# Four convolution layers on one core: layer 2's 3x3 convolution takes both halves of a tile in one 128x128 band

## The chip, the cores and the metric

The kernel runs on one core of a Trainium2 chip. TensorE (PE) does matrix products, VectorE (DVE), ScalarE (ACT) and GpSimd (POOL) do elementwise work, and SyncE (SP), ACT and GpSimd issue transfers (DMA). The metric is the device time of the whole program in microseconds (us), as a median of several executions. Times in the profile are counted from the span's start.

## The reference

The input x has 4 time steps (T), 8 channels (B), and images of 512 x 512. Four residual layers follow each other, each `x = x + f(groupnorm(x))`. Layer 0 is a spiking attention block, layer 1 a 13x13 depthwise convolution. This case is about layers 2 and 3:

```python
    def _L2_conv_ref(x, weight, bias):
        ...
        sx = MAX_Q / jnp.max(jnp.abs(x))
        sw = MAX_Q / jnp.max(jnp.abs(weight))
        qx = _quantize(x, sx)
        qw = _quantize(weight, sw)
        out_i32 = lax.conv_general_dilated(qx, qw, ..., padding=[(1, 1), (1, 1)], ...)
        out = out_i32 / (sx * sw)
        return out + bias[None, :, None, None]
    ...
    x = x + _L2_conv_ref(_gn(x), L2_conv_weight, L2_conv_bias)
    x = x + _L3_conv_ref(_gn(x), L3_conv_weight, L3_conv_bias)
```

Both are 3x3 convolutions with 8 input and 8 output channels. Layer 2 works on integers up to 127, layer 3 in float32. Between the two stands a group norm, whose statistics need the whole of layer 2's result for one time step.

## The kernel before

Layers 0 and 1 leave their result in device memory, one array for each time step, with a row of the image and a channel as its rows (`x2d`). Layers 2 and 3 run together, in `layers23`.

**Windows and tiles.** An image's 512 rows are cut into 85 windows of 8 rows that start every 6 rows (`W_IN`, `W_STEP`, `W_ALL`), so that neighbours share two rows. A window has 8 rows x 8 channels = 64 partitions, and two windows stand above each other in a tile of 128 partitions: half a = 0 and half a = 1. Two tiles (j = 0 and 1) make a pair, with four windows; `place` says where each stands: windows 4p and 4p+1 are the halves of tile j = 0, windows 4p+2 and 4p+3 the halves of tile j = 1, the even one of the latter in half 1. There are 22 pairs for a time step, and 88 in all.

**Layer 2** (`layer2`, L1051) convolves along the rows by three products, one for each horizontal tap dx, that add up in PSUM. The vertical taps and the channels are in the weights: a band matrix `band2` of 64 x 64 for each half. So each half of a tile is a product of its own, from its 64 partitions to its 64 partitions of PSUM, and of a window's 8 rows only the inner 6 come out right, as the outer two lack a neighbour. L1058 (DVE) scales the result, adds the residual and writes it to `x3`, a ring of 26 pairs in SBUF. Sums and squares for the next norm are taken on DVE (L1058's accumulator, L1069) and ACT (L1064).

**Halos** (`halos`, L1207). Before layer 3 can convolve, each window's outer rows must be overwritten by the right ones, which the neighbouring window has. For every boundary of two windows a row of 8 channels is copied in each direction, from SBUF to SBUF, by transfers that GpSimd issues. For 11 pairs (`n_chunk`) at a time, the copies of all boundaries of one kind c (c = 0 to 3: the boundary ahead of window 4p + c) are one transfer in each direction, or two where the ring wraps. They are spread over the following iterations, one or two in each.

**Layer 3** (`layer3`, L1153) is again three taps times the halves of a tile, 64 x 64, in float32, of which TensorE makes two passes each. L1162 (ACT) adds the constant, and SyncE writes the tile out (L1169). Before the products, GpSimd sets the two columns at the image's edges (L1146).

**The loop.** One iteration n loads pair n + 5 (L1002, SyncE), brings pair n + 2 into order and scales it (`normalise`: L1016 on POOL, L1020 on ACT), rounds pair n + 1 to bf16 (`quantise`: L1031 on DVE), runs layer 2 of pair n, issues halos, and runs layer 3 of pair n - 25. After a time step's last pair, `norm3` (L1104 to L1135) makes the norm's constants and layer 3's weights from the statistics, a few steps in each iteration. Buffers: six for loads (`x`), four for `u`, two for `y`, ten for outputs (`o`). SyncE's queue holds loads and outputs in one order. The order on each engine is made by a scheduler from the program's order, with `tc.issue_after` to hold layer 2 behind the normalising of later pairs and layer 3 behind layer 2.

**Weights.** `weights23` builds the bands while layer 1 runs, with small products (L891) and copies (L896).

Of the kernel before, what the change touches and what calls it, by code (L numbers as in the profile page):

```python
# [33 lines left out]
F32 = mybir.dt.float32  # L34
BF16 = mybir.dt.bfloat16
# [7 lines left out]
P = 128  # L43
T, B, N, D, H = 4, 8, 512, 512, 8
# [20 lines left out]
W_IN, W_STEP, W_ALL = 8, 6, 85  # L65
N_PAIRS = (W_ALL + 3) // 4
W2_N = 2 * N_PAIRS - 1
HALF = P // 2
# [4 lines left out]
def place(q):  # L73

    p, c = divmod(q, 4)
    return p, c // 2, (c % 2) ^ (c // 2)


def windows(k):

    p, j = divmod(k, 2)
    every = [(a, 4 * p + 2 * j + (a ^ j)) for a in range(2)]
    return [(a, q) for a, q in every if q < W_ALL]
# [43 lines left out]
def network(ctx: ExitStack, tc: tile.TileContext, i: dict, out: bass.AP):  # L127
# [115 lines left out]
    with ExitStack() as s:  # L243
        ps_1 = s.enter_context(pool("ps_2", space=PSUM))
        layer1 = Layer1(
            s, tc, x1d, x2d, avg, group_stats, r1, mr1, st2, m2, r2, most, w_sum, head, ps_1, pool
        )
        layer1.group(0)
        for g in range(1, G):
            if g == 1:  # L250
                with ExitStack() as behind:
                    for op in layer1.started:
                        behind.enter_context(tc.issue_after(op))
                    norm1(G - 1, ps_1)
                    w23 = weights23(tc, i, late, early["y"], ps_1, ident)
            layer1.group(g)
        layer1.next_norm(G - 1)
# [603 lines left out]
def weights23(tc, i, pool, scratch, ps_1, ident):  # L861


    nc = tc.nc

    def col(name, n=1):
        return pool.tile([P, n], F32, name=name)

    n_taps = 3 * B
    w = {}  # L870
    c24 = pool.tile([n_taps, i["c24"].shape[1]], F32, name="c24")
    nc.scalar.dma_start(c24, i["c24"])
    w2 = pool.tile([n_taps, n_taps], F32, name="w2t")
    nc.scalar.dma_start(w2, i["w2"])
    w3 = pool.tile([n_taps, n_taps], F32, name="w3t")
    nc.scalar.dma_start(w3, i["w3"])
    w["b2"], b3 = col("b2"), col("b3")
    nc.scalar.dma_start(w["b2"], i["b2"])
    nc.scalar.dma_start(b3, i["b3"])
    w["b23"] = col("b23")  # L880
    nc.vector.tensor_add(w["b23"], w["b2"], b3)

    def banded(taps, dtype, name, firsts):

        band = pool.tile([P, len(firsts), 3, HALF], dtype, name=name)
        for b, first in enumerate(firsts):
            ps = ps_1.tile([P, W_IN, n_taps], F32, tag="misc", name=f"ps_{name}")
            for row in range(W_IN):
                at = (W_IN - first - row) * B
                for a in range(2):  # L890
                    nc.tensor.matmul(  # L891
                        ps[a * HALF : (a + 1) * HALF, row, :], lhsT=c24[:, at : at + HALF],
                        rhs=taps, start=True, stop=True,
                    )
            for dx in range(3):
                nc.vector.tensor_copy(  # L896
                    band[:, b, dx, :].rearrange("p (r c) -> p r c", c=B),
                    ps[:, :, dx * B : (dx + 1) * B],
                )
        return band  # L900

    w["band3"] = band3 = banded(w3, F32, "band3", (-1, 1))
    w["sum3"] = pool.tile([P, 2, HALF], F32, name="sum3")
    nc.vector.tensor_add(w["sum3"], band3[:, :, 0, :], band3[:, :, 1, :])
    nc.vector.tensor_add(w["sum3"], w["sum3"], band3[:, :, 2, :])
    w["eye3"] = pool.tile([P, 2, 3, HALF], F32, name="eye3")
    nc.vector.memset(w["eye3"], 0.0)
    nc.vector.tensor_add(  # L910
        w["eye3"][:, 0, 1, B:], ident[:, : HALF - B], ident[:, HALF : P - B]
    )
    nc.vector.tensor_add(
        w["eye3"][:, 1, 1, : HALF - B], ident[:, B:HALF], ident[:, HALF + B :]
    )

    wall = scratch.tile([P, 2, D], F32, tag="y", name="wall")
    wall = wall.rearrange("p n d -> p (n d)")[:, : n_taps * n_taps]
    nc.scalar.dma_start(wall, bass.AP(i["w2"].tensor, 0, [[0, P], [1, n_taps * n_taps]]))
    w["sw"] = sw = col("sw")  # L920
    nc.vector.tensor_reduce(sw, wall, AX.X, ALU.max, apply_absolute_value=True)
    nc.vector.reciprocal(sw, sw)
    nc.vector.tensor_scalar_mul(sw, sw, MAX_Q)
    nc.vector.tensor_scalar_mul(w2, w2, sw[:n_taps])
    nc.vector.tensor_scalar(w2, w2, MAX_Q, -MAX_Q, op0=ALU.min, op1=ALU.max)
    nc.vector.tensor_scalar(w2, w2, ROUND, ROUND, op0=ALU.add, op1=ALU.subtract)
    w["band2"] = banded(w2, BF16, "band2", (0,))


    w["xq"] = [pool.tile([P, 2, D + 4], BF16, name=f"xq_{j}") for j in range(3)]  # L930
    for xq in w["xq"]:
        nc.gpsimd.memset(xq, 0.0)
    w["st3"] = [pool.tile([P, W2_N, 6], F32, name=f"st3_{j}") for j in range(2)]
    for st3 in w["st3"]:
        nc.gpsimd.memset(st3, 0.0)

    w["sums"] = [pool.tile([P, 2, W2_N], F32, name=f"sums_{j}") for j in range(2)]
    w["inv"] = col("inv")  # L940
    w["m"], w["r"] = col("m_own", T), col("r_own", T)
    w["mr"] = col("mr_own", T)
    return w


def layers23(
    s, tc, x2d, out, ident, ind, mask2, avg_same, group_steps, m2, r2, most, w, early, pool
):
    nc = tc.nc
    ps_1 = s.enter_context(pool("ps_3", space=PSUM))  # L950
# [8 lines left out]
    ps = ps_1.tile([1, P], F32, tag="misc", name="ps_most")  # L959
# [7 lines left out]
    ps = ps_1.tile([P, 1], F32, tag="misc", name="ps_top")  # L967
# [18 lines left out]
    def tiles(p):  # L986
        return [k for k in (2 * p, 2 * p + 1) if k < W2_N]

    def slot(t, p):
        return 2 * ((t * N_PAIRS + p) % RING)  # L990
# [46 lines left out]
    def by_sums(t):  # L1037
        return range(0 if t == 0 else 1, W2_N - 1, 1 if t == 0 else 2)

    def layer2(t, p):  # L1040
        ks = tiles(p)
        n_p = HALF * len(windows(ks[-1]))
        u, xq = ready.pop((t, p))
        s0 = slot(t, p)
        st3 = w["st3"][t % 2]
        for j, k in enumerate(ks):
            ps = ps_2.tile([P, D], F32, tag="conv2", name="ps_conv2")
            for dx in range(3):
                for a, _ in windows(k):
                    half = slice(a * HALF, (a + 1) * HALF)  # L1050
                    mm = nc.tensor.matmul(  # L1051
                        ps[half, :], lhsT=w["band2"][half, 0, dx, :], rhs=xq[half, j, dx + 1 : dx + 1 + D],
                        start=dx == 0, stop=dx == 2,
                    )
            own = x3[:n_p, s0 + j, 1 : D + 1]
            sums = w["sums"][t % 2][:, :, k : k + 1]
            summed = k in by_sums(t)
            done["DVE"] = nc.vector.scalar_tensor_tensor(  # L1058
                own, ps[:n_p, :], w["inv"][:n_p], u[:n_p, j, :], op0=ALU.mult, op1=ALU.add,
                accum_out=sums[:, 0, :] if summed else None,  # L1060
            ).ins
            if summed:
                square = wpool.tile([P, D], BF16, tag="square", name="square")
                done["ACT"] = nc.scalar.activation(  # L1064
                    square, own, AF.Square, bias=w["m"][:, t : t + 1], scale=-1.0,
                    accum_out=sums[:, 1, :],
                ).ins
            else:
                done["DVE"] = nc.vector.bn_stats(st3[:n_p, k, :], own).ins  # L1069
        return mm.ins  # L1070
# [3 lines left out]
    def halos(t, p0, p1):  # L1074


        for c in range(4):
            first = max(p0, 1) if c == 0 else p0
            n = min(p1, (W_ALL - c + 3) // 4) - first
            _, j, a = place(c)  # L1080
            before, j_b, a_b = place(c + 3)
            for q0, q1, n_q in split(t, first, n, before - 1):
                here = pairs[a * HALF : (a + 1) * HALF, q0 : q0 + n_q, j, :]
                there = pairs[a_b * HALF : (a_b + 1) * HALF, q1 : q1 + n_q, j_b, :]
                end = (W_IN - 1) * B
                yield here[:B], there[W_STEP * B : (W_STEP + 1) * B]
                yield there[end : end + B], here[B : 2 * B]

    def split(t, p, n, back):

        while n > 0:
            q0, q1 = slot(t, p) // 2, slot(t, p + back) // 2
            now = min(n, RING - q0, RING - q1)
            yield q0, q1, now
            n, p = n - now, p + now
# [85 lines left out]
    for n in range(n_all + N_PAIRS + LAG):  # L1181
# [20 lines left out]
        if n_chunk < n <= n_all + 3 and n % n_chunk == 3:  # L1202
            t, p = divmod(n - 3 - n_chunk, N_PAIRS)
# [4 lines left out]
        if n >= N_PAIRS + LAG:  # L1208
            t, p = divmod(n - N_PAIRS - LAG, N_PAIRS)
# [41 lines left out]
```

## Time and profile before

The median is 3003.39 us (3001.87 to 3005.93, three runs); the profiled execution spans 3002.9 us.

| what | before |
|---|---|
| PE busy, of the whole span | 2889.0 us (96%) |
| layers 2 and 3 | from about 2563 us to the end |
| layer 2's products (L1051), 64x64 bf16 | 1020, 399 ns each |
| layer 3's products (L1153), 64x64 float32 | 2040, 612 ns each |
| halo issues (L1207) on POOL | 94, 57.8 us busy |
| `u` copies (L1016), 128x512, on POOL | 168, 1187 ns each |
| quantise (L1031), 128x1024, on DVE | 84, 1131 ns each |
| packets on GpSimd's queue (q0) | 23776, 62.35 MB |

How to read it: a product's duration is its whole way through the array, so products that follow each other or stand side by side overlap, and the distance of their starts tells what they cost. A group's line gives its count, its busy time, the mean of one and the idle time ahead of it, with what ended that. The chain of waits follows the work that ended last back to its start: only what stands on it sets the time. The DMA share is the mean busy share of the core's 16 DMA engines; packets that overlap can take it above 1.

### The profile page before, as it was taken

The page shows a single profiled execution, that of the slowest core. Times are in us where ns is not written, and L with a number is a line of the kernel's source. Part 1 is how long each engine was busy: PE and PEld are TensorE (multiplying, and loading weights), DVE is VectorE, ACT ScalarE, POOL GpSimd, SP SyncE. Part 2 cuts the span into 40 slices and gives each one's busy share as a digit, 9 for nine tenths or more (in the row PEclk, how much of TensorE's full clock was granted, in tenths as well). Part 3 has the DMA queues.
Part 4 walks back from the last instruction along what each step waited for, and adds up shares of the span by engine and source line. Part 5 has one row for each costly group of instructions (what it writes and reads, how often), then busy time and mean ns, then how long its engine had stood idle before and what let it go on. Part 6 is the DMA issues. An engine that isn't in the chain of part 4 may idle for free. (4 is left out here: it accounts for less than half of the span.)

```text
span 3002.9 us, 38667 instructions
## 1 busy us (share of the span) xinstructions
PE 2889.0 (96%) x13873; PEld 1426.6 (48%) x13873; DVE 2225.3 (74%) x3875; ACT 551.0 (18%) x859; POOL 1054.3 (35%) x1971
## 2 busy tenths in 40 slices
PE   7999999999999999999999999999999999588889
PEld 3545555555555555555555555555333333244334
DVE  7887788688779868867976886786656556896660
ACT  2200000011010001001000000110112112766664
POOL 3342233233234323323422333332211112776651
PEclk9999999999999999999999999999999999889999
DMA  5311212112222222211121111112878779698886
GB/s 193 107 61 60 82 57 70 65 64 71 71 64 64 65 64 73 70 65 64 64 65 57 43 51 57 50 49 65 215 196 220 211 199 251 134 201 210 223 199 174
DMA packets 278240, 327.75 MB, mean 109 GB/s; under 512 B 23639, under 2 KB 173855, under 8 KB 277935
## 3 DMA queue, kind: packets, MB, share of 16 engines
q1 hardware_dynamic: 212304, 236.70, 28.7%
q0 software_dynamic: 23776, 62.35, 7.5%
q10 hardware_dynamic: 41967, 26.23, 3.0%
q8 instruction: 109, 1.79, 0.2%
q14 instruction: 84, 0.69, 0.1%
HBM read 210.57 MB, written 103.60 MB: 105 GB/s over the span
## 5 line engine op out<-in xcount | busy, mean ns | idle before, releaser
L485 PE MATMUL ps_in<-w_v,xn 128*128 128x512 f32 x1024 | 461.7, 600 | 2.6 <-DVE w_kq L344 2.6
L485 PE MATMUL ps_in<-xn,w_kq 128*128 128x512 f32 x1024 | 453.0, 595 | 4.8 <-DVE v_q L441 3.7
L485 PE MATMUL ps_in<-w_kq,xn 128*128 128x512 f32 x1024 | 450.1, 593 | 1.6 <-DVE v_k L450 1.6
L797 PE MATMUL ps_conv<-x,bt 112*64 112x512 f32 x2048 | 445.3, 592 | 0.8 <-ACT xo L804 0.6
L521 PE MATMUL ps_b<-toep,vtok 128*64 128x512 bf16 x3072 | 371.3, 381 | 0.0
L433 ACT ACTIVATE h_q<-v_q,c_half 128x512 f32<-128x512 f32 x96 | 69.3, 722 | 1550.4 <-DVE v_q L429 1205.7
L570 POOL COPY x1s<-x1s 128x2 f32<-128x2 f32 (+1 forms) x1024 | 227.3, 276 | 299.2 <-DVE x1s L559 299.2
L548 PE MATMUL ps_out<-wp,so 128*128 128x512 f32 x1024 | 308.4, 443 | 0.0
L458 POOL TENSOR_TENSOR h_v<-h_v,c_v 128x512 f32<-128x512 f32 x96 | 123.2, 1283 | 513.4 <-DVE h_v L457 504.4
L485 PEld LDWEIGHTS ps_in<-w_kq,xn 128*128 128x128 f32 x1024 | 194.3, 190 | 223.1 <-issue 205.3
L485 PEld LDWEIGHTS ps_in<-xn,w_kq 128*128 128x128 f32 x1024 | 192.1, 191 | 227.4 <-issue 211.8
L1153 PE MATMUL ps_conv<-x,band_t 64*64 64x512 f32 x2040 | 276.1, 612 | 24.4 <-ACT o L1162 13.8
L485 PEld LDWEIGHTS ps_in<-w_v,xn 128*128 128x128 f32 x1024 | 190.7, 191 | 215.9 <-issue 210.8
L797 PEld LDWEIGHTS ps_conv<-x,bt 112*64 112x64 f32 x2048 | 147.6, 135 | 288.6 <-issue 286.3
L521 PEld LDWEIGHTS <-vtok 128*64 128x64 bf16 x3072 | 207.7, 110 | 123.6 <-issue 2.1
L548 PEld LDWEIGHTS ps_out<-wp,so 128*128 128x128 f32 x1024 | 192.6, 188 | 94.4 <-issue 57.8
L1016 POOL COPY u<-x 128x512 f32<-128x512 f32 (+1 forms) x172 | 198.2, 1185 | 104.5 <-DMA x<-x 56.7
L559 DVE SCALAR_TENSOR_TENSOR x1s<-v_p,xr 128x256 f32<-128x256 f32 x256 | 187.1, 771 | 16.2 <-DMA x<-x1s 5.2
L195 POOL TENSOR_TENSOR grstd_x<-grstd_x,neg_half 128x1 f32<-128x1 f32 (+1 forms) x28 | 21.3, 762 | 473.5 <-DVE grstd_x L194 473.5
L815 POOL DMA_DIRECT2D x<-xo x128 | 71.4, 565 | 312.4 <-ACT xo L804 298.1
L1153 PEld LDWEIGHTS ps_conv<-x,band_t 64*64 64x64 f32 x2040 | 112.3, 136 | 135.9 <-issue 94.2
L1051 PE MATMUL ps_conv<-xq,band 64*64 64x512 bf16 x1020 | 138.8, 399 | 32.1 <-DVE xq L1031 32.0
(182 smaller groups left out, 3580.4 us busy)
## 6 DMA issues: line engine op xcount, KB each, us to landing
x<-x SPq DMA_DIRECT2D x64, 917.0 KB
x<-x SPq DMA_DIRECT2D x168, 256.0 KB
x<-x1s POOLq DMA_DIRECT2D x128, 262.0 KB, 2.5
x<-in_x SPq DMA_DIRECT2D x128, 256.0 KB
xr<-in_x SPq DMA_DIRECT2D x128, 256.0 KB
out<-o SPq DMA_DIRECT2D x164, 192.0 KB
xs<-in_x SPq DMA_DIRECT2D x112, 256.0 KB
x<-xo ACTq DMA_DIRECT2D x128, 128.0 KB
```

The lines of the kernel that those rows point to most:

```text
L433: nc.scalar.activation(h, v, AF.Identity, bias=c_col, scale=0.5)
L458: nc.gpsimd.tensor_add(h, h, c_twice[n])
L485: mm = nc.tensor.matmul(ps, lhsT=lhsT, rhs=rhs, start=k == 0, stop=k == NC - 1)
L521: nc.tensor.matmul(pb[two * DH : (two + 1) * DH, :], lhsT=v[:, c, h * DH : (h + 1) * DH], rhs=toep[z][:, h, u : u + N], start=c == 0 and z ...
L548: nc.tensor.matmul(ps, lhsT=so[:, k, c * P : (c + 1) * P], rhs=wpT[z][:, k, :], start=k == 0 and z == 0, stop=k == NC - 1 and z == 1,)
L559: nc.vector.scalar_tensor_tensor(own, v.rearrange("p (g v) -> p g v", g=PH)[:, two, :], 1.0, by_phase[:, two, :], op0=ALU.is_ge, op1=ALU.add,)
L570: nc.gpsimd.tensor_copy(x1[:, f, u : u + n], x1[:, fm, um - n + 1 : um + 1][:, ::-1])
L797: mm = nc.tensor.matmul(ps[q * M1 : (q + 1) * M1, :], lhsT=bt[:, z, :], rhs=xt[:, w0 : w0 + N_PS1, z : z + NV], start=z == 0, stop=z == SH ...
L815: engine.dma_start(bass.AP(dst.tensor, dst.offset + (q * n_half * W1_OUT * B + b) * D + f * NV, [[B * D, W1_OUT], [W1_OUT * B * D, n_half] ...
L1016: nc.gpsimd.tensor_copy(u[:n_p, j, :].rearrange("p (v g) -> p v g", g=PH), x[:, j, :].rearrange("p (g v) -> p v g", g=PH),)
L1051: mm = nc.tensor.matmul(ps[half, :], lhsT=w["band2"][half, 0, dx, :], rhs=xq[half, j, dx + 1 : dx + 1 + D], start=dx == 0, stop=dx == 2,)
L1153: mm = nc.tensor.matmul(ps[j][b * HALF : (b + 1) * HALF, :], lhsT=band[half, b, dx, :], rhs=x3[half, s0 + j, dx : dx + D], start=dx == 0, ...
```

## The change

The weights of layer 2 become one band of 128 x 128 for each kind of tile (j = 0 and 1). Its diagonal blocks are the old 64 x 64 band, and the blocks beside the diagonal hold the taps by which the rows at the boundary of a tile's two halves see each other. A tile then takes one product of 128 x 128 for each dx instead of two of 64 x 64, and the boundary inside a tile comes out right without a copy. Copies are left for c = 0 and c = 2 alone: the boundaries between tiles. To make room, the taps and the old band now stand in a scratch tile (`parts`), and the new band is put together by more copies and four small products.

```diff
-    def banded(taps, dtype, name, firsts):
-
-        band = pool.tile([P, len(firsts), 3, HALF], dtype, name=name)
+    def banded(taps, band, name, firsts):
...
-    w["band2"] = banded(w2, BF16, "band2", (0,))
+    w["band2"] = band2 = pool.tile([P, 2, 3, P], BF16, name="band2")
+    nc.gpsimd.memset(band2, 0.0)
+    inner = banded(w2, inner.rearrange("p (b x m) -> p b x m", b=1, x=3), "inner2", (0,))
+    nc.vector.tensor_copy(below, w2)
+    nc.vector.memset(below[: 2 * B, :], 0.0)
+    ps = ps_1.tile([P, 2, n_taps], F32, tag="misc", name="ps_outer2")
+    for a in range(2):
+        half = slice(a * HALF, (a + 1) * HALF)
+        at = (W_IN - W_STEP) * B
+        nc.tensor.matmul(
+            ps[half, 0, :], lhsT=c24[:B, at : at + HALF], rhs=w2[:B, :], start=True, stop=True
+        )
+        at = (W_STEP + 1) * B
+        nc.tensor.matmul(
+            ps[half, 1, :], lhsT=c24[:, at : at + HALF], rhs=below, start=True, stop=True
+        )
+    for a in range(2):
+        half = slice(a * HALF, (a + 1) * HALF)
+        nc.vector.tensor_copy(
+            band2[half, :, :, half],
+            inner[half, 0, :, :].unsqueeze(1).to_broadcast([HALF, 2, 3, HALF]),
+        )
+        for j in range(2):
+            at = (1 - a) * HALF + (0 if j == a else HALF - B)
+            nc.vector.tensor_copy(
+                band2[half, j, :, at : at + B],
+                ps[half, 0 if j == a else 1, :].rearrange("p (x c) -> p x c", c=B),
+            )
...
             for dx in range(3):
-                for a, _ in windows(k):
-                    half = slice(a * HALF, (a + 1) * HALF)
-                    mm = nc.tensor.matmul(
-                        ps[half, :], lhsT=w["band2"][half, 0, dx, :], rhs=xq[half, j, dx + 1 : dx + 1 + D],
-                        start=dx == 0, stop=dx == 2,
-                    )
+                mm = nc.tensor.matmul(
+                    ps[:n_p, :], lhsT=w["band2"][:n_p, j, dx, :n_p],
+                    rhs=xq[:n_p, j, dx + 1 : dx + 1 + D], start=dx == 0, stop=dx == 2,
+                )
...
     def halos(t, p0, p1):
...
-        for c in range(4):
+        for c in (0, 2):
```

More of the change, by code (lines that the diff above doesn't have):

```diff
@@ L870, in weights23 @@
     w = {}
-    c24 = pool.tile([n_taps, i["c24"].shape[1]], F32, name="c24")
+    parts = scratch.tile([P, 2, D], F32, tag="y", name="parts")
+    c24 = parts[:n_taps, 0, : i["c24"].shape[1]]
     nc.scalar.dma_start(c24, i["c24"])
-    w2 = pool.tile([n_taps, n_taps], F32, name="w2t")
+    w2, w3, below = (parts[:n_taps, 1, j * n_taps : (j + 1) * n_taps] for j in range(3))
     nc.scalar.dma_start(w2, i["w2"])
-    w3 = pool.tile([n_taps, n_taps], F32, name="w3t")
     nc.scalar.dma_start(w3, i["w3"])
+    inner = parts[:, 1, P : P + 3 * HALF // 2].bitcast(BF16)
     w["b2"], b3 = col("b2"), col("b3")
@@ L900, in banded @@
         return band
-    w["band3"] = band3 = banded(w3, F32, "band3", (-1, 1))
+    band3 = pool.tile([P, 2, 3, HALF], F32, name="band3")
+    w["band3"] = banded(w3, band3, "band3", (-1, 1))
     w["sum3"] = pool.tile([P, 2, HALF], F32, name="sum3")
```

## The prediction

> **What bounds the kernel now.** I read the page's forty slices first, then the chain of waits in order of time, the groups by shape, the waits and some windows of the last third; only layers 2 and 3 are touched, and they run from 2563 us to the end. The slices:
>
> ```profile
> PE   7999999999999999999999999999999999588889
> DMA  5311212112222222211121111112878779698886
> ```
>
> Up to slice 34 TensorE is full; after it, PE has gaps and the transfers are near full. The chain, in order of time:
>
> ```profile
> 2653.53 2.58 PE ps_conv L1153 x22
> 2656.10 1.08 PE ps_conv L1051 x10
> 2657.19 0.21 PE ps_conv L1153
> 2657.40 2.58 PE ps_conv L1153 x22
> ...
> 2692.56 22.85 DMA out<-o x3
> ```
>
> From 2650 to 2692 the chain is TensorE alone, one pair of tiles every 2657.40 - 2653.53 = 3.87 us. Then it jumps to output transfers. The columns below are us, busy PE, PEld, DVE, ACT and POOL with their counts, granted clock, DMA share, GB/s:
>
> ```profile
> 2570.00:2600.00 30.00, 19.84 (x152) 8.19 (x150) 27.89 (x59) 28.69 (x57) 26.59 (x22) 0.94 0.60 159
> 2600.00:2630.00 30.00, 16.52 (x107) 6.16 (x104) 29.00 (x48) 25.73 (x51) 25.32 (x27) 0.85 1.00 149
> 2647.00:2692.00 45.00, 44.77 (x418) 22.18 (x418) 43.06 (x64) 36.57 (x59) 39.84 (x53) 0.98 1.04 208
> 2715.00:2930.00 215.00, 185.91 (x1586) 88.98 (x1586) 142.41 (x272) 139.35 (x223) 134.84 (x183) 0.95 0.87 210
> ```
>
> So there are four stretches. A, to 2650: layer 2 alone, ACT and DVE full. B, 2650 to about 2715: PE full, while transfers already take a share of 1.04 and fall behind. C, 2715 to 2930: the timeline of L1058 shows pairs 43 to 87, so 215 / 45 = 4.78 us a pair against PE's 3.87, and PE is idle for 29 us. D, the last 73 us: layer 3 alone on PE. What ends the waits in C (the waits of 2700 to 2930: total, times, longest):
>
> ```profile
> ACT o L1162 <- DMA out<-o: 64.2, 37, 6.3
> POOL u L1016 <- DMA x<-x: 44.7, 21, 6.0
> ```
>
> ACT waits for an output buffer to be written out, POOL for an input to land: C is bound by transfers.
>
> **What the halo copies cost.** The packet records of C, by queue: 1344 packets of 4096 B on GpSimd's queue (the halos), 557 ns each; 18998 of 2048 B on SyncE's queue (loads, outputs), 111 ns each. 1344 x 557 ns = 749 us; 18998 x 111 ns = 2109 us; the whole is 0.87 x 16 x 215 = 2993 us. Halos are 13% of the bytes but 25% of the time. The 2048 B packets take 152 ns in 2647:2692, where the share is 1.04, and 104 ns after 2940, with few halos.
>
> **What the Trainium skill says.** "DMA: Bandwidth & Descriptors", section "Issuing engines are not separate DMA queues": transfers of all issuing engines share the same 16 engines and interleave. The slower 2048 B packets beside halos agree. "SBUF — State Buffer", section "Who interferes with whom": a DVE instruction in a two-port mode and a GpSimd instruction exclude each other. The trace agrees; quantise takes 0.68 us when POOL is idle, 1.06 us beside its copies, and more when a halo issue has put POOL behind:
>
> ```profile
> 2610.05 3.28 DVE L1031 TENSOR_SCALAR xq<-y 128x1024 bf16<-128x1024 f32 x1 [0.18 <-ACT y L1020]
> 2614.59 0.68 DVE L1031 TENSOR_SCALAR xq<-y 128x1024 bf16<-128x1024 f32 x1
> ```
>
> "TensorEngine Tiling (Array Packing)", section "Key Properties": changing the tiling mode drains TensorE. The trace shows this at a norm, where a 128x128 product stands between 64x64 ones:
>
> ```profile
> 2732.03 1.03 PE L1051 MATMUL ps_conv<-xq,band 64*64 64x512 bf16 x8
> 2732.99 0.38 PE L178 MATMUL gps_x<-gsum_x,avg_same 128*128 128x1 f32 x2
> 2733.30 0.66 PE L1153 MATMUL ps_conv<-x,band_t 64*64 64x512 f32 x4
> ```
>
> Two 64x64 products run side by side every 0.215 us, so the last two of the eight start at 2732.03 + 3 x 0.215 = 2732.68; L178 starts 0.31 later instead of 0.215: 0.09 us for the switch.
>
> **The change, part by part.**
>
> 1. Layer 2 on PE. Before: 12 products of 64x64 a pair, two side by side, 6 x 0.215 = 1.29 us (the chain's 1.08 + 0.21). After: 6 full products, 6 x 0.215 = 1.29 us. No full bf16 product over 512 columns is in the trace. The nearest, L501 (128x128 bf16 over 128 columns), starts every 0.054 us, so its weights hide; L548 (f32 weights) takes 1.86 / 8 = 0.2325 us. Bounds 0.215 and 0.2325; I take 0.215, as bf16 weights hide. Zero here.
>
> 2. Mode switches, added. The built order keeps layer 2's 6 products and layer 3's 12 in turns, so each pair switches from 64x64 to 128x128 and back: 2 x 0.09. After a switch the first weights are not hidden: L1153's first product takes 0.641 instead of 0.588 us after L178 (+0.05); I take 0.03 to 0.05 for bf16. Together 0.26 to 0.28; bounds 0.2 and 0.4. Layer 2's first pairs have no layer 3 between them. It concerns pairs 25 to 87, where PE's floor becomes 3.87 + 0.28 = 4.15 us. In B (17 pairs) nothing hides it: +5 us. In C it adds 45 x 0.28 = 12.6 us, where 29 us of idle can take it.
>
> 3. Halos. Of 94 copies (10752 KB: 84 boundaries, two directions, 16 KB each, four time steps) 50 remain (5376 KB). In C this takes 749 / 2 / 16 = 23 us off each DMA engine: 187 - 23 = 164 us busy for 45 pairs, 3.6 us a pair at a share of 1. At C's share of 0.87 that is 4.2 us, about PE's new floor. C's bounds: 45 x 4.15 = 187 us if nothing else waits, 215 if the waits have another cause. In C before, the excess over the larger floor (187 us of transfers) was 28 us; after, the larger floor is PE's 187 and transfers have 23 us to spare, so I take half of that excess, 13 us: 200 us, 15 less than 215.
>
> 4. A. In the first chunk 4 instead of 8 halos are issued. The pair's period there is 2.54 us without halos and 9.28 for three pairs with them, so 1.66 us lost three times; I count one fewer: 1.7. The first norm begins with L1104, which waits 3.6 us behind POOL's copies and a halo issue (its neighbours of the same shape take 0.25): 3.3 back. In the new order DVE interleaves the norm with pairs 22 and 23, but then waits on PE and POOL in a row: about -0.5. Sum 4.5, bounds 0 and 7.
>
> 5. POOL's order. Edges (L1146), one a pair before, now stand in batches of up to 18 ahead of copies, some behind a halo's landing (6.7 us by the page's issues). The same work, but three bursts of some 4 us and a wait of up to 4 us each. Behind them stand the u copies, then ACT's y, quantise, layer 2. POOL is 135 of 215 us busy and works two pairs ahead, so I charge 1 us each, 3 in all; bounds 0 and 12.
>
> 6. Set-up. Four small products, six copies, a memset and a copy of the taps, in layer 1. The products cost PE under 0.3 us; DVE has idle time there (about 30 busy of 50 us), and L759's last three bands come 13.9 us (one image of L797) before PE needs them. Zero.
>
> D is untouched. Sum: A -4.5, B +5, C -15, POOL +3: -11.5, so 2992.
>
> **The rivals.** (a) Transfers get out of the way wholly: C falls to 187 us, POOL costs nothing, A gives 4.5: 3003.4 - 28 + 5 - 4.5 = 2976. For it: B before ran at PE's floor despite a share of 1.04, and halos come in bursts that buffers can take up. Against: norms at pairs 43 and 65 stall DVE anyway, and PE's products run at half speed for some us after an idle time. (b) The gains cancel: C gains only 4, which pays for B less A, and POOL 3: 3003. For it: loads and outputs stay (0.62 of the share of 0.87). (c) Slower: SyncE issues loads and outputs in one order, each waiting for buffers, so C's waits may be a matter of that order; then C keeps its 215, B pays 5, POOL up to 10, A gives 4.5: 3003.4 + 5 + 10 - 4.5 = 3014; with a switch at 0.4 us somewhat more. For it: SyncE's own waits are for ACT and POOL, not for transfers. Against: the share above 1 and the 557 ns packets.
>
> **How the numbers follow.** The main case (2982 to 2997) has 0.47, (a) 0.18, (b) 0.2, (c) 0.15. Faster by 0.2% means below 2997.4: main and (a), 0.65. Same: 0.2. Slower: 0.15. The range reaches from just above (a)'s floor, 2977, into (c), 3009.
>
> **What would show it.** Right: layer 2 as some 504 products of 128*128 (the four time steps' last tiles stay half) with nearly the duration of before and PE's chain near 4.15 us a pair in B; 50 halo issues; share in C near 0.85; waits of L1162 for out clearly under 64 us; L1104 under 1 us. Wrong: a period near 3.9 in B (switches cheap: faster than forecast), or C still at 4.7 us a pair with half the halos (transfers were not it).

## The result, and the profile after

| kernel | median us | lowest to highest | ratio to before, 95% interval |
|---|---|---|---|
| before | 3004.66 (4 runs) | 3001.87 to 3011.84 | |
| after | 2992.15 (4 runs) | 2990.54 to 2996.51 | 0.9957 [0.9936, 0.9978] |

The changed kernel is faster by 0.43%; the profiled executions span 3002.9 and 2991.6 us. Lines have moved by 29 or 31: L1051 is now L1080 (layer 2's products), L1153 L1182 (layer 3's), L1016 L1047 (`u` copies), L1020 L1051 (ACT's scaling to `y`; the number that layer 2's products had before), L1031 L1062 (quantise), L1058 L1087 (residual), L1104 L1133 (the norm's first step), L1146 L1175 (edges), L1162 L1191 (output), L1207 L1236 (halo issues).

Where the difference lies is seen from the starts of each pair's first L1058 or L1087 in the timeline (us; in brackets us a pair):

| stretch | before | after | difference | forecast |
|---|---|---|---|---|
| to pair 0 | 2571.24 | 2574.66 | +3.4 | 0 |
| A: pairs 0 to 25, layer 2 alone | 79.58 | 77.70 | -1.9 | -4.5 |
| B: pairs 25 to 43, PE full | 71.65 | 74.39 | +2.7 | +5 |
| C: pairs 43 to 87 | 207.66 (4.72) | 192.05 (4.36) | -15.6 | -15, and +3 for POOL's order |
| D: from pair 87 on, layer 3 alone | 72.81 | 72.81 | 0 | 0 |

The 3.4 us ahead of pair 0 are there in full after layer 0's second image (289.08 against 292.53 us), where both kernels do the same work, and the seven other kernels below that build the new band reach pair 0 at 2570.64 to 2575.26. So it varies from run to run and is not put down to the change. In layers 2 and 3 alone the profiles differ by -1.9 + 2.7 - 15.6 = -14.8 us.

The page's slices, after:

```profile
PE   7999999999999999999999999999999999689999
DMA  5312222222222221212221111111877778698865
```

Of the four slices near the end that stood at 8 before, three are at 9 now: TensorE is full to the end but for the norms. The windows of A's end and of C (us, busy PE, PEld, DVE, ACT, POOL with their counts, granted clock, DMA share, GB/s):

```profile
2647.00:2692.00 45.00, 43.72 (x301) 14.26 (x308) 38.67 (x58) 32.52 (x53) 38.68 (x58) 0.95 0.97 211
2715.00:2930.00 215.00, 205.38 (x1446) 68.65 (x1465) 170.63 (x294) 144.07 (x233) 134.99 (x178) 0.99 0.79 198
```

In C, PE is idle for 215 - 205.4 = 9.6 us where it was idle for 29, and the transfers' share has gone from 0.87 to 0.79 although more pairs pass in the same time. From pair 43 to pair 87 alone, where the shares are 0.79 and 0.86, a pair takes 0.79 x 192.05 / 44 = 3.4 us of each DMA engine, before 0.86 x 207.66 / 44 = 4.1. In the packet records of the window there are 751 packets of 4096 B on GpSimd's queue (1344 before), 555 ns each (557).

The chain of waits in order of time (start us, us), in C, before and after:

```profile
2792.38 6.85 DMA out<-o
2799.24 5.45 DMA out<-o
2806.25 8.00 DMA out<-o
```

```profile
2857.34 2.74 PE ps_conv L1182 x24
2860.07 1.41 PE ps_conv L1080 x6
2861.48 2.74 PE ps_conv L1182 x24
...
2929.22 54.03 PE ps_conv L1182 x498
```

In 2715 to 2930 before, the chain went through output transfers for 31.7% of the time and through loads for 13.9%. Now, as far back as it can be followed in C (to 2841 us), it has no transfer: it is TensorE but for a norm, one pair every 2.74 + 1.41 = 4.15 us (by the starts, 4.14); against B's rows before (2.58 + 1.08 + 0.21) the 24 products of layer 3 up to the first of layer 2 take 0.16 us more, and layer 2's up to the next of layer 3 take 0.12 more. Layer 2's products by shape (count, busy us, mean ns, idle time ahead):

```profile
L1080 PE MATMUL ps_conv<-xq,band 128*128 128x512 bf16 x470 | 129.9, 402 | 29.0 <-DVE xq L1062 26.3 <-issue 1.0
```

A full product passes the array in 402 ns, a half-size one in 399 before, and six of them replace twelve. (Of the 504 full products the trace has kept 470.) The waits of 2700 to 2930 (total us, times, longest):

```profile
ACT o L1191 <- PE ps_conv L1182: 18.0, 12, 2.9
...
POOL u L1047 <- DMA x<-x: 3.1, 1, 3.1
```

L1191's wait for an output buffer (64.2 us before) is gone; ACT now waits for products. The wait of the `u` copies for a transfer fell from 44.7 to 3.1. DVE in stretch A, from the timeline:

```profile
2604.14 3.38 DVE L1062 TENSOR_SCALAR xq<-y 128x1024 bf16<-128x1024 f32 x1
...
2613.50 3.30 DVE L1062 TENSOR_SCALAR xq<-y 128x1024 bf16<-128x1024 f32 x1 [0.17 <-ACT y L1051]
...
2630.67 0.65 DVE L1133 TENSOR_SCALAR sums<-sums 128x42 f32<-128x42 f32 x1
2631.23 1.60 DVE L1062 TENSOR_SCALAR xq<-y 128x1024 bf16<-128x1024 f32 x1
...
2634.43 1.98 DVE L1136 TENSOR_SCALAR sums<-sums,m_own 128x42 f32<-128x42 f32 x1
```

The norm's first step takes 0.65 us instead of 3.62, as forecast. But a later step of it, L1136, now takes 1.98, and quantise is still held up three times (a third one of 2.30 us follows).

### The profile page after: what moved, and what is told of

Its sections match the earlier page's. It is cut to its first block, busy times and chain, and to the rows that moved or that the text cites. A ratio compares the mean times of both kernels' runs of the same rounds, so it can differ in the third digit from the quotient of the medians.

```text
span 2991.6 us, 37579 instructions
## 1 busy us (share of the span) xinstructions
PE 2900.4 (97%) x13343; PEld 1391.5 (47%) x13377; DVE 2243.8 (75%) x3883; ACT 550.0 (18%) x859; POOL 1035.6 (35%) x1928
## 5 line engine op out<-in xcount | busy, mean ns | idle before, releaser
L797 PE MATMUL ps_conv<-x,bt 112*64 112x512 f32 x2048 | 445.1, 592 | 0.1
L797 PEld LDWEIGHTS ps_conv<-x,bt 112*64 112x64 f32 x2048 | 146.1, 135 | 288.4 <-issue 286.7
L1182 PE MATMUL ps_conv<-x,band_t 64*64 64x512 f32 x2040 | 246.4, 599 | 3.1 <-DVE band_t L1151 3.1
L1047 POOL COPY u<-x 128x512 f32<-128x512 f32 (+1 forms) x172 | 208.7, 1247 | 95.8 <-issue 48.5
L804 ACT ACTIVATE xo<-ps_conv,off 128x512 f32<-128x512 f32 x128 | 87.7, 687 | 430.6 <-PE ps_conv L797 316.0
L458 POOL TENSOR_TENSOR h_k<-h_k,c_k 128x512 f32<-128x512 f32 x96 | 122.8, 1279 | 116.4 <-DVE h_k L457 116.4
```

The source lines that it names most:

```text
L458: nc.gpsimd.tensor_add(h, h, c_twice[n])
L797: mm = nc.tensor.matmul(ps[q * M1 : (q + 1) * M1, :], lhsT=bt[:, z, :], rhs=xt[:, w0 : w0 + N_PS1, z : z + NV], start=z == 0, stop=z == SH ...
L804: nc.scalar.activation(xo[:, a, :], ps, AF.Identity, bias=off[:, t : t + 1])
L1047: nc.gpsimd.tensor_copy(u[:n_p, j, :].rearrange("p (v g) -> p v g", g=PH), x[:, j, :].rearrange("p (g v) -> p v g", g=PH),)
L1182: mm = nc.tensor.matmul(ps[j][b * HALF : (b + 1) * HALF, :], lhsT=band[half, b, dx, :], rhs=x3[half, s0 + j, dx : dx + D], start=dx == 0, ...
```

## The experiments

**The theory** is that of the prediction: C was bound by transfers; half the halos let PE's floor become the limit, and the switches between the 64x64 and the 128x128 mode raise that floor by 0.27 us a pair and so give back part of the gain. **The rivals**: that the full product itself, or the order of SyncE's queue, and not the switch, sets the new pace; that the number of halos does not matter; that halos are harmful by where they are issued.

### Half the halos, with products of the old size

```diff
 # before.py
     def halos(t, p0, p1):
...
-        for c in range(4):
+        for c in (0, 2):
```

It leaves the rows at the boundary inside a tile without their neighbours' values.

> The kernel before with its 64x64 products of layer 2, but with the halo copies of c = 0 and 2 alone; the rows at the boundary inside a tile are left wrong. So it has the changed kernel's transfers without its mode switches. Theory (half the halos frees the DMA engines, and the switches cost PE 0.27 us a pair): PE's floor is 3.87 us a pair again, the transfers need 3.6 at a share of 1, so some waits stay: 3.9 to 4.1 us a pair in 2715 to 2930, 2975 to 2984 us in all, 8 to 17 below the changed kernel. Rival (the gain came from the full-size products, not from the copies left out): about the time before, 2999 to 3006 us, and 4.7 us a pair.

Measured: 2977.47 us (2970.78 to 2980.34), ratio 0.9901 [0.9886, 0.9917]; span 2972.1. Its window of C and its chain:

```profile
2715.00:2930.00 215.00, 205.14 (x1839) 111.49 (x1832) 160.68 (x285) 148.48 (x238) 131.96 (x183) 0.98 0.80 206
```

```profile
2880.53 2.57 PE ps_conv L1153 x22
2883.11 1.08 PE ps_conv L1051 x10
...
2884.41 2.58 PE ps_conv L1153 x22
```

PE's pace in C's quiet pairs is 2884.41 - 2880.53 = 3.88 us, and the stretch takes 180.87 us (4.11 a pair). Stretch A is 77.70 us and D 72.78, as in the changed kernel; B is 69.85 against 74.39, C 180.87 against 192.05. So the halved halos alone bring 1.0%, and the full-size band takes more than half of it back: in B, (74.39 - 69.85) / 18 = 0.25 us a pair. The chain in C is free of transfers here too, as far back as it can be followed.

One thing goes with the number of halos: the scheduler also orders GpSimd's work anew. The edges, one at a time before, stand in batches of up to 19. Before, PE waited 7.8 us in 2700 to 2930 for edges (L1146), and here it does not. No run changes that order alone; the next one speaks against it as the cause, since its waits for edges are short as well (0.7 us).

### The full-size band, with all halos

```diff
 # after.py
     def halos(t, p0, p1):
...
-        for c in (0, 2):
+        for c in range(4):
```

> The changed kernel with all four kinds of halo copies issued; those inside a tile write rows that are right already. So it has the mode switches and the old transfers. Theory: transfers bound it as before, 4.7 us a pair from 2715 on, and the stretch to 2715 runs at 4.15 us a pair instead of 3.87: 3003 to 3012 us. Rival (the copies were not what the waits were for, the gain came from the products or from the new order): 2990 to 2996 us.

Measured: 3007.2 us (3002.9 to 3014.63), ratio 1.0005 [0.9998, 1.0012]. The window of C and the waits of 2700 to 2930:

```profile
2715.00:2930.00 215.00, 203.12 (x1386) 67.42 (x1383) 155.52 (x283) 142.18 (x229) 140.59 (x186) 0.97 0.88 215
```

```profile
ACT o L1191 <- DMA out<-o: 41.1, 23, 4.7
POOL u L1047 <- DMA x<-x: 33.9, 12, 5.9
```

The transfer waits are back, with a share of 0.88, and transfers hold 41.1% of the chain in 2715 to 2930 (45.6% before). In total the larger products cost nothing here, but that is a sum of unlike parts: B takes 74.22 us, as in the changed kernel and 2.6 more than before, D takes 4.3 more after a late last norm, and C takes 200.43 us (4.56 a pair, below the 4.7 expected), 7.2 less than before with as many halos. Why C is shorter was not tried; PE's waits for edges, 7.8 us before and 0.7 here, are of that size. That PE's extra work lies in time it would have waited for transfers is the reading that fits, not a thing measured by itself. With the run before it, all four combinations are known:

| ratio to before | all halos | half the halos |
|---|---|---|
| products of 64x64 | 1 | 0.9901 |
| products of 128x128 | 1.0005 | 0.9957 |

The change's two halves do not add up. The larger band costs 0.05% with all halos, where transfers set C's pace, and 0.56% with half of them, where PE does.

### No halos at all

```diff
 # after.py
-        for c in (0, 2):
+        for c in ():
```

It leaves every tile's outer rows without their neighbours' values.

> The changed kernel with no halo copies at all; the outermost rows of the tiles are left wrong. Theory (with half the copies PE alone bounds pairs 25 to 87, at 4.15 us): nothing to gain there; the stretch of layer 2 alone loses its three stalls of quantise, 2 to 4 us: 2987 to 2991 us, DMA share near 0.7. Rival (the transfers that are left still cost time between the pairs): 2982 us or less.

Measured: 2989.03 us (2987.6 to 2990.84), ratio 0.9944 [0.9931, 0.9957]. C's window:

```profile
2715.00:2930.00 215.00, 208.11 (x1485) 69.18 (x1485) 163.10 (x294) 144.40 (x232) 120.07 (x154) 0.98 0.64 181
```

The share falls to 0.64, and C stays at 190.58 us (4.33 a pair) against 192.05. So after the change the halo copies no longer limit C. What is left over PE's 44 x 4.14 = 182 us lies at the norms: with halos, pairs 43 to 51 take 37.10 us and 64 to 73 take 43.23, together 80.3, and PE's floor for these 17 is 70.4: that is the whole 9.9 us; without halos it is much the same (37.50 and 41.35). The other pairs keep to 4.14 on average. What PE waits for there, in the changed kernel from 2700 to 2930, are the norm's statistics and layer 3's new weights, 8.2 of C's 9.6 us of idle time:

```profile
PE gps_x L178 <- DVE gsum_x L175: 5.1, 3, 2.2
PE ps_conv L1182 <- DVE band_t L1151: 3.1, 2, 1.5
```

A goes from 77.70 us to 76.13, less than the 2 to 4 expected: the first 20 pairs gain 4.4 us, as no quantise there is longer than 1.14, and the next five, at the first norm, lose 2.8.

### Two pairs in turn: half the switches

Layer 2 of two pairs, then layer 3 of two pairs, in every second iteration:

```diff
 # after.py
-            with ExitStack() as order:
-                for op in (first, then, *behind):
-                    order.enter_context(tc.issue_after(op))
-                did = layer2(*divmod(n, N_PAIRS))
+            if n % 2:
+                with ExitStack() as order:
+                    for op in (first, then, *behind):
+                        order.enter_context(tc.issue_after(op))
+                    for m in (n - 1, n):
+                        did = layer2(*divmod(m, N_PAIRS))
...
-        if n >= N_PAIRS + LAG:
-            t, p = divmod(n - N_PAIRS - LAG, N_PAIRS)
-            with tc.issue_after(did):
-                behind = (layer3(t, p, *norms[t]),)
+        if n >= N_PAIRS + LAG and n % 2:
+            for m in (n - N_PAIRS - LAG, n - N_PAIRS - LAG + 1):
+                t, p = divmod(m, N_PAIRS)
+                with tc.issue_after(did):
+                    behind = (layer3(t, p, *norms[t]),)
```

> The changed kernel with layer 2 of two pairs and then layer 3 of two pairs in every second iteration, so that TensorE changes its mode half as often; same work, same copies. Theory (0.27 us of PE's 4.15 a pair are two mode switches): 8.0 us for two pairs on PE, 62 x 0.135 = 8 us less than the changed kernel, 2983 to 2987 us, if the coarser order makes no new waits (up to 4 us). Rival (the full-size products themselves are slower than two of half size side by side, 1.41 against 1.29 us): no gain, 2992 us or above.

Measured: 2992.81 us (2990.68 to 2994.1), ratio 0.9957 [0.9944, 0.997]. The total was missed; it lies where the rival put it. The chain in C shows that the rival is wrong all the same:

```profile
2851.63 5.31 PE ps_conv L1182 x48
2856.94 2.71 PE ps_conv L1080 x12
2859.64 5.32 PE ps_conv L1182 x48
```

Two pairs take 5.31 + 2.71 = 8.02 us instead of 2 x 4.14 = 8.28. One way there and back saved is 0.26 us, with the same products: it is the switch that costs, not the product. For a pair without switches this gives (2 x 8.02 - 8.28) / 2 = 3.88, which is the pace of the half-size kernel. C took 184.77 us, 7.3 less. But A took 85.15 us instead of 77.70. DVE there, from the timeline:

```profile
2596.56 1.52 DVE L1062 TENSOR_SCALAR xq<-y 128x1024 bf16<-128x1024 f32 x1 [0.98 <-ACT y L1051]
...
2602.98 0.74 DVE L1062 TENSOR_SCALAR xq<-y 128x1024 bf16<-128x1024 f32 x1 [0.76 <-ACT y L1051]
```

In A there is no switch to save, as layer 3 has not begun, and DVE and ACT are full. With two pairs together DVE does four residuals in a row, then waits for ACT's `y` before it can quantise: 11.1 us of idle time ahead of L1062 from 2570 to 2660, against 3.2 in the changed kernel.

### Two pairs in turn, from layer 3's start on

So the same, but only from pair 24 on, where layers 2 and 3 alternate:

```diff
 # after.py, on top of the last
+            alone = n < N_PAIRS + 2
-            if n % 2:
+            if alone or n % 2:
...
-                    for m in (n - 1, n):
+                    for m in (n,) if alone else (n - 1, n):
```

> The changed kernel with two pairs of layer 2 and two of layer 3 at a time, as in the run before, but only from pair 24 on, where layer 3 runs too; up to pair 23 layer 2 goes pair by pair. Theory (the run before saved 7 us on TensorE from pair 43 on and lost as much in layer 2's first 25 pairs, where no mode switch is saved and the coarse order delays DVE and ACT): both are had, 2983 to 2987 us, 8.0 us for two pairs. Rival (the loss belongs to the coarse order wherever it stands): 2991 us or above.

Measured: 2984.73 us (2983.93 to 2985.65), ratio 0.9931 [0.9918, 0.9945]. A is 77.06 us, C 186.03. The chain:

```profile
2854.47 5.31 PE ps_conv L1182 x48
2859.79 0.32 PE ps_conv L1080
2860.11 0.05 issue
2860.17 2.33 PE ps_conv L1080 x10
2862.49 5.31 PE ps_conv L1182 x48
```

The pace is 2862.49 - 2854.47 = 8.02 us for two pairs again, and the loss of A is gone, as expected. Nothing of the computation is left out in this version, and it is faster than both kernels: 0.69% under before, where the change alone has 0.43%.

### Halos issued by ScalarE

Does GpSimd's issuing of halos cause the long quantises of A?

```diff
 # after.py
-            nc.gpsimd.dma_start(*copies.pop(0))
+            nc.scalar.dma_start(*copies.pop(0))
```

> The changed kernel with its 50 halo copies issued by ACT instead of GpSimd; same bytes. Theory (the stalls of quantise of 2.3 to 3.4 us in layer 2's first pairs come from the issue on GpSimd, which puts its copies behind, and not from the transfers themselves): quantise takes 1.1 us at most there, the first 25 pairs gain 3 to 5 us, the rest is PE's 4.14 us a pair, 2986 to 2990 us. Rival (the transfers make the stalls, or ACT, full in that stretch, pays for the issues): 2992 us or above.

Measured: 2993.12 us (2990.49 to 2995.27), ratio 0.9959 [0.9947, 0.9971]: no gain over the changed kernel. The long quantises are gone (1.1 to 1.2 us in their place), so it was GpSimd's issues and not the transfers that made them. But A is only 0.7 us shorter, where 3 to 5 were expected. ScalarE's queue (ACTq) and DVE:

```profile
2609.10 0.79 ACTq L1236 DMA_DIRECT2D x<-x  x1
...
2616.19 0.73 ACTq L1236 DMA_DIRECT2D x<-x  x1
2616.96 1.24 ACT L1051 ACTIVATE y<-u,mr_own,r_own 128x1024 f32<-128x1024 f32 x1 [4.37 <-DMA x<-x]
...
2618.24 0.70 DVE L1062 TENSOR_SCALAR xq<-y 128x1024 bf16<-128x1024 f32 x1 [4.73 <-ACT y L1051]
```

The second halo issue starts 7.1 us after the first; the profile puts ACT's idle time down to the landing of a halo or load, and the `y` that every engine waits for stands behind it in ACT's order: that pair takes 6.75 us. B takes 75.92 us, 1.5 more. And 3.3 us are lost at the end, where the last norm comes late: from pair 87 on 76.14 us against 72.81, with PE idle for 1.6 us and at a granted clock of 0.89 and 0.94 in the twenty us from 2915 (1.00 in the changed kernel). So the cause of A's stalls was found, and moving the issues to ACT only exchanges them for another wait.

### Halos issued by SyncE

```diff
 # after.py
-            nc.gpsimd.dma_start(*copies.pop(0))
+            nc.sync.dma_start(*copies.pop(0))
```

> The changed kernel with its 50 halo copies issued by SyncE, in one order with loads and outputs. Theory of GpSimd's issue: quantise's stalls go, as with ACT, without costing ACT time: 2985 to 2990 us. Rival: a halo copy at the head of SyncE's queue waits for layer 2's rows, and loads and outputs wait behind it: new waits for inputs, 2995 us or above.

Measured: 3033.73 us (3029.48 to 3036.06), ratio 1.0093 [1.008, 1.0107]. The waits of 2700 to 2930:

```profile
DVE xq L1062 <- ACT y L1051: 74.1, 17, 7.6
POOL u L1047 <- DMA x<-x: 54.9, 17, 7.1
```

The long quantises of A are gone here too (1.1 us), but B takes 83.04 us and C 228.96, 5.20 a pair, although the share is 0.69. The time is the rival's; its mechanism is not what the trace shows. SyncE's halo issues wait 1.6 us in all in this window, and the `u` copies do wait for loads, but transfers are only 1.9% of the chain from 2715 to 2930. In the slow places it runs from layer 3's products through ACT's output and the next `y` to the quantise and layer 2's products:

```profile
2867.42 0.69 ACT o L1191
2868.12 1.25 ACT y L1051
2869.40 0.70 DVE xq L1062
2870.14 1.99 PE ps_conv L1080 x6
```

The edit also changed the order that the scheduler gave ACT: the `y` of pair 34 stands behind 18 outputs here and behind 12 in the changed kernel. How much of the loss belongs to this order and how much to late loads stays open. So this run does not show that the order of SyncE's queue alone can set C's pace.

### Both: two pairs in turn, halos issued by ScalarE

The edit of the two-pair order from layer 3's start on, with `nc.scalar` for the halos.

> Both: two pairs at a time from pair 24 on, and the halo copies issued by ACT. If the two add up: 2978 to 2984 us. If ACT's issues collide with the outputs of two pairs in a row: no better than two pairs alone, 2985 us or above.

Measured: 2989.78 us (2988.53 to 2992.26), ratio 0.9949 [0.9937, 0.9962]. The two do not add up; the time is that of the second expectation. Against two pairs from layer 3's start on alone, A is 0.7 us shorter (76.32), as it was with ACT's issues alone, but B rises from 74.95 to 77.20 us and C from 186.03 to 190.81. In 2715 to 2930 the chain goes through transfers again for 13.2% of the time; what holds them up was not followed. Two pairs with GpSimd's issues stay the best.

## Why the prediction was right

2992.0 us was forecast, 2992.15 measured: the mechanism was right, and the closeness of the total is partly luck. The terms of layers 2 and 3 add up to -4.5 + 5 - 15 + 3 = -11.5 us as forecast, and to -14.8 in the profiles. Errors of about 2.5 us in A and in B went opposite ways, and POOL's 3 us were not seen. In the profiles the 3.4 us ahead of pair 0, which vary from run to run, hide the remainder; the medians differ by 12.5.

**Part 1, layer 2 on PE, zero: right.** A product takes 402 ns against 399, full products that follow each other start 0.215 to 0.227 us apart, and a pair takes (2 x 8.02 - 8.28) / 2 = 3.88 us once the switches are taken out.

**Part 2, the switches, 0.26 to 0.28 us a pair: right.** 4.14 less 3.88 is 0.26, and the two-pair order gives 0.26 again. The Trainium skill, "TensorEngine Tiling (Array Packing)", section "Key Properties", says that a change of mode drains TensorE; these runs put the price of there and back at 0.25 to 0.26 us. The records of the single products split it, at the pair that starts at 2857 us. Layer 2's first product starts 0.54 us after layer 3's last four, which follow each other every 0.43 (+0.11), and layer 3's first start 0.31 us after layer 2's last instead of 0.215 (+0.09); 2 x 0.09 was forecast. Layer 3's first four then hold PE for 0.48 us instead of 0.43 (+0.05, as forecast), and layer 2's first product costs 0.01 more instead of 0.03 to 0.05. But the +0.05 does not belong to the change of mode alone: before, too, layer 3's first products take 0.64 us where no mode changes (2656.82 us). There they stood beside layer 2's last ones, and the pair still took 3.87.

The step "in B nothing hides it: +5 us" was half wrong. The switches did cost 74.39 - 69.85 = 4.5 us there, but B before was not at PE's floor throughout: with halos halved and products of the old size it goes from 71.65 to 69.85. So 1.8 us of waits fell away in the same stretch, and +2.7 was left.

**Part 3, C -15: the size right, its reason partly.** The transfers got their relief (751 packets for 1344, 4.1 to 3.4 us a pair), and the limit moved from them to PE, as forecast. It came from fewer packets, not from faster ones: the prediction took the slower 2048 B packets beside halos as a sign of the shared engines, but from pair 43 to pair 87 these take 112 ns before, 118 after and 115 with no halos at all. And "I take half of that excess" supposed that transfers would still cause the other 13 us. The halos do not: without any C is only 1.5 us shorter. The 9.9 us that remain over PE's floor lie at the norms at pairs 43 and 65, which stood in the text as an argument against rival (a) and not in the sum. Rival (a) was right that transfers get out of the way, and wrong on the total since it let C fall to 187 us and gave A its whole 4.5.

**Part 4, A -4.5: too much, -1.9.** L1104's 3.6 us went to 0.65 as forecast. What failed is "I count one fewer" stall: four halo issues instead of eight still gave three long quantises (3.38, 3.30 and 2.30 us against 3.33, 3.28 and 2.90), so that 0.6 us was saved and not 1.7. And the new order's loss, put at 0.5, was larger: L1136, now beside POOL's copies, took 1.98 us where the same step (L1107) took 0.25 before. The sum 0.6 + 3.0 - 1.7 = 1.9 us agrees with what was measured, though no run took these steps apart.

**Part 5, POOL's order +3: not seen.** In C the edges (L1175) waited for a transfer once, 1.7 us, and with PE as the limit and POOL two pairs ahead, nothing of it reached the chain.

**Part 6 and D: right.** D is 72.81 us in both. From layer 1's first product (L797) to pair 0, the stretch that holds the set-up, it is 465.2 us before and 464.7 after.

**Rivals (b) and (c)** fell with the result: C lost 15.6 us, where (b) gave it 4 and (c) none. Halving the halos alone brings 1%, and the chain of before, with its 45.6% of transfers against 6.3% for SyncE's issue of loads, says why.

## What to carry to other kernels

Copies that are few by bytes can be many by transfer time: here 13% of the bytes took 25% of it, so look at the time their packets take in the records, and at the next limit (here PE at 3.88 us a pair, and the norms), which says how much of a saving can be kept. A larger matmul that is free by itself may cost a mode switch on each side of it. That cost did not show in the total while transfers set the pace, and showed as soon as they did not; running two pairs of each layer in turn halves it. Apply such an order only in the stretch that has the switches, as elsewhere the longer bursts break up a balanced DVE and ACT. Moving an issue to another engine also changes the order of that engine's work, so look at that order before the transfer is blamed.

## What the runs showed of the hardware

- **A switch from 64x64 float32 to 128x128 bf16 products and back cost 0.25 to 0.26 us**, in three comparisons: 4.14 against 3.88 us a pair, 8.02 against 8.28 for two pairs, and 4.5 us over 18 pairs in B.
- **A quantise was held up over several of GpSimd's copies in a row.** The Trainium skill, "SBUF — State Buffer", section "Who interferes with whom", says that between a DVE instruction in a two-port mode and a GpSimd instruction, whoever issues first has the shared ports for the whole instruction. The wait here was longer than one. In the changed kernel GpSimd issues a halo at 2602.10 and then runs four copies from 2602.84 to 2606.95; the quantise that starts at 2604.14 lasts 3.38 us, to 2607.52, so its own 0.68 us (its time beside an idle POOL) begins at 2606.84, when all four copies are about over and not after the one that was running. Where ScalarE or SyncE issues the halos the quantises at that place take 1.1 us; with ScalarE eight copies then stand in 9.64 us, 1.2 each instead of 1.03. That it is the closer row of copies after an issue that keeps DVE out is a reading of these records; a direct experiment was not made.
- **PE's granted clock fell to about half after some idle times and not after others.** In the kernel before, PE sat idle for some 3 us at two places in C and then ran the same 24 products of layer 3:

```profile
2764.37 4.50 PE L1153 MATMUL ps_conv<-x,band_t 64*64 64x512 f32 x24 [3.02 <-POOL x L1146]
2872.06 2.81 PE L1153 MATMUL ps_conv<-x,band_t 64*64 64x512 f32 x24 [3.22 <-POOL x L1146]
```

  The granted clock of the 3.4 us that follow is 0.53 the first time and 1.00 the second. With ScalarE's issues an idle time of only 1.60 us (to 2922.64) is followed by 0.53, which is part of the 3.3 us that the end loses there. So the length of the idle time alone does not decide it in these traces; what does was not tried.
